# Moving weight preparation on GpSimd: into the f and v loop, and behind the first image's value sums

## The chip, the cores and the metric

The kernel runs on one core of a Trainium2 chip. The metric is the device time of one execution in microseconds (us). The engines are named as in the profile: PE is TensorE's matrix products, PEld its weight loads, DVE is VectorE, ACT is ScalarE, POOL is GpSimd and SP is SyncE, whose queue issues most of the DMAs. Each engine works through its own queue of instructions in the order in which the program issued them.

## What is computed

The input is four images of 256 channels and 64 x 64 points, in float32. Two layers follow each other. The reference, cut to what matters here:

```python
# layer 0: attention over the 4096 points of an image
attn = softmax(einsum('bnd,bdm->bnm', q, k), axis=-1)
x = gamma[0] * einsum('bcn,bmn->bcm', v, attn) + x

# layer 1, cluster: f and v are 1x1 convolutions of the normed image to 96 channels,
# folded into 2 x 2 quarters of 4 heads, 4 centres in each
cn = cen * rsqrt((cen * cen).sum(-1) + 1e-12)
pn = pts * rsqrt((pts * pts).sum(-1) + 1e-12)      # pts are the points of f
sim = sigmoid(beta + alpha * einsum('bmc,bnc->bmn', cn, pn))
mask = one_hot(argmax(sim, axis=1))                # one centre for each point
sim = sim * mask
agg = (einsum('bmn,bnc->bmc', sim, v2) + v_cen) / (mask.sum(-1) + 1.0)
y = x + ls1 * conv1x1(einsum('bmn,bmc->bnc', sim, agg), proj_w)

# layer 1, the multilayer part
hdn = conv1x1(gelu(conv1x1(group_norm(y), mlp_w1)), mlp_w2)   # 256 -> 1024 -> 256
y = y + ls2 * hdn
z = relu(batch_norm(y * dw_w))
z = relu(batch_norm(conv1x1(z, pw_w)))
```

## The kernel before

The order of the work is written out by hand: the whole body stands under `tc.manual_schedule()` (line 2052), so each engine receives its instructions in the order in which the Python code issues them. Waits between engines are placed by what reads and writes which tile.

Several matrix products are done with fewer multiplications, by seven products of quarters in place of eight. This needs sums and differences of the quarters of both factors. Those of the weights are made by POOL, in place where the room allows it:

- `turn_mlp` (line 248) does two instructions on the first weights of the multilayer part, tile `w1`: it adds the quarter D to C (line 251) and multiplies D by -1 (line 252).
- `turn_w2` (line 1622) does three on the second weights, tile `w2`: lines 1627, 1629 and 1631. The results w7 and s2 go to buffers of the tags `rden` and `q`; s1 overwrites a quarter of `w2` in the first three images and has a buffer of its own in the last.
- The last step of `load_rest` (line 176) does two on `wpw_s`, the weights of the closing convolution (lines 188 and 189).

For an image the work runs in this order:

1. `alone` (line 865), for the first image only: projections, the scores of the first block of points, and the values v in pairs (`v_pair`). `added(g)` issues four POOL sums over v each, through the helper at line 664. The generator `load_rest` is stepped from u = 3 on: its first four steps issue the DMAs of the remaining weights on SP's queue, the fifth is the subtraction in `wpw_s`. Behind the loop follow `added(5)`, `added(6)`, `exps(0)`, `factors(0)`, `added(7)`. `exps(u)` subtracts the maximum on DVE and takes the exponential on ACT; `factors(u)` makes sums of quarters of the exponentials, one on DVE (line 678, tile t) and the others on POOL (line 664, tiles s, t and acc).
2. `weighting`: 64 units of scores times values. POOL and DVE make the sums of quarters, TensorE multiplies (line 734). Near its end `load_mlp` issues the DMAs of w1 and w2 on SP's queue. In the last image `turn_mlp` is called right at its end.
3. `cluster` (line 1140). After the group norm comes the f and v loop (line 1319) over eight blocks of 512 points. For each, TensorE makes f and v (line 1331) in one of two PSUM buffers, DVE moves them to SBUF with their bias (line 1341) and the similarities too (line 1350). `heads(nb - 1)` squares f of the block before on POOL (line 1310; for the last block line 1308) and sums the squares on DVE (line 1312). In the loop's block 6 the first half of the similarities is finished (`similar(0)`).
4. Behind the loop DVE works through the two halves of the masks: `affine` (line 1268), `largest` (lines 1273 to 1281), `weights` (line 1286), with `similar(1)` in between (line 1261). `fill(n)` hands TensorE pieces of other work meanwhile, the value projections of the next image (line 443) or, in the last image, the last block of the image before. Then TensorE sums the values by masks (`summed`, line 1366), the counts follow, and `turn()` is called at line 1398, which is five POOL instructions, or three in the last image. Behind it in the code stand the transposes (line 1412), two small POOL memsets (1423, 1424) and the product named gp (line 1434).
5. `mlp`: the multilayer part, which reads what `turn()` made.

The call that the change moves, and the one that steps `load_rest`:

```python
        summed(lambda j, q: sim[:, j, q, :], False)
        count(0)
        count(1)
        turn()
...
                if u > 2:
                    next(rest, None)
```

Of the kernel before, what the change touches and what calls it, by code (L numbers as in the profile page):

```python
# [11 lines left out]
ALU = mybir.AluOpType  # L12
# [48 lines left out]
def attention_then_cluster_block(  # L61
# [17 lines left out]
    nc = tc.nc  # L79
# [168 lines left out]
    def turn_mlp():  # L248

        _, w_cd, _, w_d = own_w["q"]  # L250
        nc.gpsimd.tensor_tensor(w_cd, w_cd, w_d, ALU.add)
        nc.gpsimd.tensor_scalar(w_d, w_d, -1.0, None, ALU.mult)

    def roots():
        for s, v in ((dw_d, "dw_v"), (pw_s, "pw_v")):
            rsqrt(s, par(v), BN_EPS)
        table(AF.Exp)
# [80 lines left out]
    def attention(b, xs, ys):  # L338
# [54 lines left out]
        def staged():  # L393

            st = spool.tile([P, 4, NB], F32R, tag="s", name=f"st_{b}")
            ps = ps_s.tile([P, 2, NB], F32, tag="s", name=f"pr_{b}")
            k0, q0 = (st[:, 0], st[:, 1]), (st[:, 2], st[:, 3])
            for j, w in enumerate("kq"):  # L400
                projected(w, 0, ps[:, j])
            halves_of("k", *k0, ps[:, 0])
            k_straight(0, k0)
            qs[0] = work.tile([P, NB], F32R, tag="q", name=f"q_{b}_0")
            halves_of("q", *q0, ps[:, 1])
            straight("q", 0, qs[0], *q0, nc.scalar)
            for u in range(1, 4):
                k_straight(u, k0)
            return k0, q0
# [43 lines left out]
        def v_pair(i):  # L453
            for j in range(2 * i, 2 * i + 2):
                for k in range(KC):
                    v_step(j, k)
# [408 lines left out]
        def alone():  # L865

            roots()
            for i in range(2):
                v_pair(i)
            k0, q0 = staged()  # L870
            for i in range(2, 5):
                v_pair(i)

            def added(*gs):
                for g in gs:
                    for f in sums(g):
                        f()

            added(0, 1)
            rest = load_rest()  # L880
            for u in range(GRP):
                half(u, 0)()
                if u < GRP - 1:
                    half(u, 1)()
                else:

                    sc = products(u, 1)
                    highest_of(0, tiles(sc))
                    kept(u, 1, sc)
                if u == 0:  # L890
                    k1 = halved("k", 1, False)
                    for i in range(4, GRP):
                        k_straight(i, k1)
                elif u == 1:
                    q1 = halved("q", 1, False)
                else:
                    v_pair(u + 3)
                    if u % 2 == 0:
                        added(u // 2 + 1)
                if 1 < u < 6:  # L900
                    written("kqkq"[u - 2], (u - 2) // 2, *(k0, q0, k1, q1)[u - 2], nc.gpsimd)
                if u == 3:
                    q_block(1)
                    k_unit(GRP)
                if u > 2:
                    next(rest, None)
            fold(0)
            v_pair(11)
            added(5)
            tp = turned_over(0, ps_m.tile([P, 4, P], F32, tag="m", name=f"tt_{b}_0"))  # L910
            half(GRP, 0)
            v_pair(12)
            dgs["dg"] = across(0, "w2", tp)
            v_pair(13)
            added(6)
            spread(0, dgs["dg"])
            v_pair(14)
            wf()
            exps(0)
            factors(0)  # L920
            v_pair(15)
            half(GRP, 1, True)
            added(7)
            for _ in rest:
                pass
# [32 lines left out]
        def weighting(next_x, fill, early, begin):  # L958
# [125 lines left out]
            for _ in range(4):  # L1084
                next(quarters)
            if b == B - 1:
                turn_mlp()
            table(AF.Sqrt)
            ends = b == B - 1
            fill(1 if ends else 2)  # L1090
# [49 lines left out]
    def cluster(b, ys, stats, cells, rest, fill, gelu, nxt, maxima, turn):  # L1140
# [161 lines left out]
        def heads(nb, between=lambda: None):  # L1302

            fh, o = nb // 4, nb % 4
            f = vf[nb // 2][:, nb % 2, :, :ED]
            for g in range(2) if nb == NBLK - 1 else ():
                h = f[:, 2 * g : 2 * g + 2]
                nc.gpsimd.tensor_tensor(h, h, h, ALU.mult)
            if nb < NBLK - 1:
                nc.gpsimd.tensor_tensor(f, f, f, ALU.mult)  # L1310
            between()
            nc.vector.tensor_reduce(
                prns[fh].rearrange("p (q j h) -> p q j h", q=2, j=8)[:, :, 2 * o : 2 * o + 2],
                f.rearrange("p (g j) (h e) -> p g j h e", g=2, h=HEADS),
                AX.X,
                ALU.add,
            )

        for nb in range(NBLK):
            fh, o = nb // 4, nb % 4  # L1320
            if 1 < nb + 1 < NBLK:
                norm(nb + 1)
            if nb in later:
                later[nb]()
            xn = xns.pop(nb)

            ps = ps_s.tile([P, 2, 2, C], F32, tag="s", name=f"fv_{b}_{nb}")
            for j in range(4):
                g = j // 2
                for k in range(KC):  # L1330
                    nc.tensor.matmul(  # L1331
                        ps[:, g, j % 2, : 2 * ED + 16],
                        xn[:, k, j * P : (j + 1) * P],
                        mix[:, k, fh, 16 * g : 16 * g + 2 * ED + 16],
                        start=(k == 0),
                        stop=(k == KC - 1),
                    )
            if nb == NBLK - 1:
                heads(nb - 1)
            for g in range(2):  # L1340
                nc.vector.tensor_tensor(
                    vf[nb // 2][:, nb % 2, 2 * g : 2 * g + 2, :],
                    ps[:, g, :, 16 - 16 * g : 16 - 16 * g + 2 * ED],
                    fvb.unsqueeze(1).to_broadcast([P, 2, 2 * ED]),
                    ALU.add,
                )
            for g in range(2):
                q = 2 * fh + g
                d0 = 2 * ED * g
                nc.vector.tensor_tensor(  # L1350
                    folded(sgs[fh])[:, g, 2 * o : 2 * o + 2],
                    ps[:, g, :, d0 : d0 + 16],
                    dot_b[:, q * 16 : (q + 1) * 16].unsqueeze(1).to_broadcast([P, 2, 16]),
                    ALU.add,
                )
            if 0 < nb < NBLK - 1:
                heads(nb - 1)
            if nxt and nb == 2:
                nxt.queries()

        agg_p = ps_a.tile([P, NB], F32, tag="a0", name=f"agg_{b}")

        def summed(w, first):
# [31 lines left out]
        summed(lambda j, q: sim[:, j, q, :], False)  # L1395
        count(0)
        count(1)
        turn()

        cnt_p = ps_a.tile([P, NB], F32, tag="a1", name=f"cnt_{b}")  # L1400
        nc.tensor.matmul(cnt_p[:ED, :64], ones[:, :ED], bests[0], start=True, stop=True)
# [217 lines left out]
        t = own_w["w2"]  # L1619
        return t[:, :h_n, :P], t[:, h_n:, :P], t[:, :h_n, P:], t[:, h_n:, P:]  # L1620

    def turn_w2(b, kept):


        a11, _, a21, a22 = quarters_w2()
        w7 = work.tile([P, h_n, P], F32, tag="rden", bufs=1, name=f"w2_7_{b}")
        nc.gpsimd.tensor_tensor(w7, a21, a11, ALU.subtract)
        s1 = work.tile([P, h_n, P], F32, tag="q", name=f"w2_1_{b}") if kept else a21
        nc.gpsimd.tensor_tensor(s1, a21, a22, ALU.subtract)
        s2 = work.tile([P, h_n, P], F32, tag="q", name=f"w2_2_{b}")  # L1630
        nc.gpsimd.tensor_tensor(s2, s1, a11, ALU.subtract)
        return s1, s2, w7

    def mlp(b, ys, stats2, fill, nxt, blocks, turned, maxima):

# [416 lines left out]
    with tc.manual_schedule():  # L2052
        here = attention(0, xs0, [])
        here.alone()
        late = None
        for b in range(B):
            xs1 = []
            nxt = attention(b + 1, xs1, []) if b + 1 < B else None

            def next_x():  # L2060
                if nxt:
                    xs1.append(load_x(b + 1, len(xs1)))

            begin, todo, gelu = late or (
                lambda: None,
                list(nxt.projections) if nxt else [],
                lambda i: None,
            )
            fill = filler(todo)
            stats, cells, rest = here.weighting(  # L2070
                next_x, fill, [] if b else derived(), begin
            )
            turned = []

            def turn():
                if nxt:
                    turn_mlp()
                turned.extend(turn_w2(b, not nxt))

            maxima = []  # L2080
            stats2 = cluster(b, here.ys, stats, cells, rest, fill, gelu, nxt, maxima, turn)

            late = mlp(b, here.ys, stats2, fill, nxt, NBLK - (b == B - 2), turned, maxima)
            here = nxt
# [76 lines left out]
```

## Time and profile before

| | |
|---|---|
| median of three runs | 3128.08 us (3124.45 to 3131.26) |
| profiled execution, its own time | 3132.96 us |
| its span in the profile | 3131.2 us |
| mean granted clock of TensorE | 0.994 |
| PE busy | 3052.7 us (97%) |
| DVE busy | 2513.3 us (80%) |
| POOL busy | 2330.7 us (74%) |
| ACT busy | 1780.1 us (57%) |
| `turn()`, five POOL instructions, image 0 | 565.93 to 572.96 us, 1.26 to 1.54 us each |
| the subtraction in `wpw_s`, two POOL instructions | 58.62 to 59.72 us |

A row of a timeline gives the start in us, the duration in us, the engine, the line of the kernel, the operation, what it writes and reads, the shapes, and how many instructions are merged in it; a bracket at the end gives the idle time of the engine just before it and who ended it. A row of the waits gives who waited for whom, the total in us, how often, and the longest. A row of the chain of waits gives start, duration, engine, tile and line of one piece of the chain that ended last. Rows of stages give the stage, its length, and the busy time and number of instructions of PE, PEld, DVE, ACT and POOL, then the granted clock of TensorE as a share of full speed, the DMA share and GB/s.

### The profile page before, as it was taken

What the parts mean: (1) busy time and instruction counts of PE and PEld (TensorE: products, weight loads), DVE (VectorE), ACT (ScalarE), POOL (GpSimd) and SP (SyncE); (2) the same over time, 40 slices, a digit from 0 to 9 for tenths busy, and PEclk for the clock granted to TensorE, in tenths of its full rate; (3) what the DMA queues carried; (4) which work ended last, traced back from release to release, by engine and by line L of the source; (5) the groups of instructions that cost most, each with busy time, mean ns of one, the idle gap of its engine ahead of it and who ended that gap; (6) DMA issues with size and microseconds to landing.
All of it is one profiled execution on the core that took longest, in us unless ns stands there. A gap on an engine that the chain in (4) does not pass through costs nothing.

```text
span 3131.2 us, 41360 instructions
## 1 busy us (share of the span) xinstructions
PE 3052.7 (97%) x14210; PEld 2498.0 (80%) x14210; DVE 2513.3 (80%) x3548; ACT 1780.1 (57%) x2817; POOL 2330.7 (74%) x2243
## 2 busy tenths in 40 slices
PE   8999999999999999999999999999999999999999
PEld 5788887788688888878868888886877888875886
DVE  4999888777798888877779888877768988887675
ACT  5666664544566666454556666645446666655444
POOL 5888886477588888657758888955766988893563
PEclk9999999999999999999999999999999999999999
DMA  5112226100112113510011212440011112150000
GB/s 174 47 56 64 61 90 168 58 18 28 48 47 68 55 61 111 157 44 26 19 58 44 68 61 64 117 144 34 28 41 44 59 57 67 55 153 1 14 21 28
DMA packets 105570, 200.40 MB, mean 64 GB/s; under 512 B 14880, under 2 KB 30864, under 8 KB 103824
## 3 DMA queue, kind: packets, MB, share of 16 engines
q1 hardware_dynamic: 100464, 178.66, 17.9%
q0 software_dynamic: 4256, 18.90, 2.9%
q8 instruction: 113, 1.85, 0.2%
q14 instruction: 97, 0.79, 0.1%
q10 hardware_dynamic: 640, 0.20, 0.0%
HBM read 147.01 MB, written 48.34 MB: 62 GB/s over the span
## 4 chain that ended last, share of the span: by engine, by line
PE 73%; DVE 9%; POOL 9%; issue 3%; ACT 3%; DMA 2%; SPq 1%; POOLq 0%; ACTq 0%; DVEq 0%
PE av L734 34%; PE mo L1771 10%; PE sc L489 7%; PE hq L1854 5%; PE hp L1854 3%; PE hr L1854 3%; PE fv L1331 3%; POOL acc L664 3%; POOL t L664 2%; DVE top L513 2%; DVE s L655 2%; PE vp L443 2%; POOL s L664 1%; PE mo L1755 1%; PE hq_pw L1854 1%
## 5 line engine op out<-in xcount | busy, mean ns | idle before, releaser
L502 ACT COPY s<-sc 128x1024 f32<-128x1024 f32 x512 | 515.2, 1012 | 426.3 <-PE sc L489 418.2
L655 DVE TENSOR_TENSOR s<-s,hold 128x1024 f32<-128x1024 f32 x512 | 598.5, 1209 | 9.9 <-ACT hold L638 6.0
L664 POOL TENSOR_TENSOR acc<-acc,t 128x512 f32<-128x512 f32 x408 | 541.9, 1348 | 0.0
L734 PE MATMUL av<-s,sum 128*128 128x256 f32 x2048 | 527.1, 380 | 5.5 <-POOL s L664 5.3
L734 PE MATMUL av<-t,v 128*128 128x256 f32 x2048 | 527.2, 380 | 2.5 <-POOL t L664 2.4
L734 PE MATMUL av<-s,v 128*128 128x256 f32 x2048 | 525.7, 379 | 2.5 <-ACT t L764 1.3
L664 POOL TENSOR_TENSOR s<-t,s 128x512 f32<-128x512 f32 x256 | 341.9, 1336 | 221.9 <-DVE t L678 154.9
L678 DVE TENSOR_TENSOR t<-s,hold 128x1024 f32<-128x1024 f32 x256 | 311.7, 1217 | 189.4 <-POOL acc L664 98.1
L513 DVE TENSOR_TENSOR top<-sc,top 128x1024 f32<-128x1024 f32 x350 | 426.6, 1219 | 21.4 <-ACT s L502 17.6
L734 PEld LDWEIGHTS av<-s,v 128*128 128x128 f32 x2048 | 387.3, 189 | 65.0 <-ACT xn L1722 2.3
L734 PEld LDWEIGHTS av<-s,sum 128*128 128x128 f32 x2048 | 387.7, 190 | 63.7 <-POOL s L664 11.4
L734 PEld LDWEIGHTS av<-t,v 128*128 128x128 f32 x2048 | 387.4, 190 | 63.4 <-POOL t L664 8.9
L1809 ACT ACTIVATE hs<-hs,pv_s 128x256 f32<-128x256 f32 x496 | 232.6, 503 | 353.2 <-DVE hs L1845 353.2
L489 PE MATMUL sc<-q,k 128*128 128x512 f32 x1024 | 392.8, 468 | 20.0 <-ACT s L502 9.6
L1771 PE MATMUL mo<-hs,w 128*128 128x256 f32 x1512 | 385.0, 381 | 0.0
L664 POOL TENSOR_TENSOR t<-s 128x512 f32<-128x512 f32 x256 | 330.3, 1290 | 45.4 <-PE av L734 31.8
L1771 PEld LDWEIGHTS mo<-hs,w 128*128 128x128 f32 x1512 | 283.7, 190 | 47.3 <-ACT hs L1809 6.2
L659 ACT ACTIVATE hold<-s 128x512 f32<-128x512 f32 x256 | 154.2, 602 | 214.9 <-DVE s L655 214.7
L1845 DVE TENSOR_TENSOR hs<-hq,hs 128x256 f32<-128x256 f32 x496 | 198.5, 421 | 86.6 <-PE hq L1854 76.2
L661 ACT ACTIVATE s<-s 128x1024 f32<-128x1024 f32 x256 | 266.9, 1043 | 0.0
L734 PE MATMUL av<-t,sum 128*128 128x256 f32 x1024 | 262.4, 378 | 0.0
L489 PEld LDWEIGHTS sc<-q,k 128*128 128x128 f32 x1024 | 174.2, 189 | 108.2 <-DVE top L513 59.1
(292 smaller groups left out, 4878.5 us busy)
## 6 DMA issues: line engine op xcount, KB each, us to landing
k<-k SPq DMA_DIRECT2D x248, 256.0 KB, 2.7
x<-in_x SPq DMA_DIRECT2D x62, 512.0 KB, 6.9
out<-xn SPq DMA_DIRECT2D x62, 256.0 KB, 2.1
att<-t SPq DMA_DIRECT2D x56, 256.0 KB, 4.0
x<-att POOLq DMA_DIRECT2D x12, 1024.0 KB, 9.9
w<-in_w SPq DMA_DIRECT2D x8, 1024.0 KB, 11.8
q<-q SPq DMA_DIRECT2D x31, 256.0 KB, 4.1
rden<-row_rd SPq DMA_DIRECT2D x28, 256.0 KB, 3.7
```

The lines of the kernel that those rows point to most:

```text
L489: nc.tensor.matmul(sc[:, r, :], k_s[:, (2 * h + r) * P : (2 * h + r + 1) * P], qs[u // GRP], start=True, stop=True,)
L502: nc.scalar.copy(slots[u][:, PAIR[h]].rearrange("p h r n -> p r h n"), tiles(sc))
L513: nc.vector.tensor_tensor(top, src, top if saved[nb] is None else saved[nb], ALU.max)
L655: nc.vector.tensor_tensor(sh, sh, mb.to_broadcast([P, 2, 2, QW]), ALU.subtract)
L661: nc.scalar.activation(s[:, PAIR[1]], s[:, PAIR[1]], AF.Exp)
L664: nc.gpsimd.tensor_tensor(out, x, y, op)
L678: nc.vector.tensor_tensor(t31[u], s[:, B11 : B22 + 1 : 2], b12.to_broadcast([P, 2, 2, QW]), ALU.add)
L734: nc.tensor.matmul(av[bank][:, half_ * QW : (half_ + 1) * QW], a[:, r], t[:, r], start=(g == 0 and r == 0 and i in (1, 7, 2, 4)), stop=(g ...
L1771: return nc.tensor.matmul(bank[:, half * HB : (half + 1) * HB], a[:, j], t, start=start, stop=stop)
L1809: nc.scalar.activation(src, src, AF.Gelu_apprx_tanh, bias=pvc("b1", P, j + 4 * (i > 1)))
L1845: nc.vector.tensor_tensor(dst, ps, term, ALU.add)
L1854: nc.tensor.matmul(out, w, x, start=True, stop=True)
```

## The change

`turn_mlp` and `turn_w2` become generators that yield after each POOL instruction. `cluster` makes one generator of both ahead of the f and v loop and takes one step of it behind `heads(nb - 1)` in the blocks 1 to 6; what is left is run out behind the loop, and the call behind the counts is gone. The last image's call of `turn_mlp` at the end of `weighting` stays where it was. In `alone`, `load_rest` is stepped four times in place of five, so that the subtraction in `wpw_s` is issued by the loop at the end of `alone`, behind `added(7)`. No instruction is added or taken away.

```diff
--- before.py
+++ after.py
@@ -248,8 +248,8 @@
     def turn_mlp():
 
         _, w_cd, _, w_d = own_w["q"]
-        nc.gpsimd.tensor_tensor(w_cd, w_cd, w_d, ALU.add)
-        nc.gpsimd.tensor_scalar(w_d, w_d, -1.0, None, ALU.mult)
+        yield nc.gpsimd.tensor_tensor(w_cd, w_cd, w_d, ALU.add)
+        yield nc.gpsimd.tensor_scalar(w_d, w_d, -1.0, None, ALU.mult)
 
     def roots():
         for s, v in ((dw_d, "dw_v"), (pw_s, "pw_v")):
@@ -902,8 +902,8 @@
                 if u == 3:
                     q_block(1)
                     k_unit(GRP)
-                if u > 2:
-                    next(rest, None)
+                if 2 < u < 7:
+                    next(rest)
             fold(0)
             v_pair(11)
             added(5)
@@ -1084,7 +1084,8 @@
             for _ in range(4):
                 next(quarters)
             if b == B - 1:
-                turn_mlp()
+                for _ in turn_mlp():
+                    pass
             table(AF.Sqrt)
             ends = b == B - 1
             fill(1 if ends else 2)
@@ -1316,6 +1317,8 @@
                 ALU.add,
             )
 
+
+        turning = turn()
         for nb in range(NBLK):
             fh, o = nb // 4, nb % 4
             if 1 < nb + 1 < NBLK:
@@ -1355,9 +1358,12 @@
                 )
             if 0 < nb < NBLK - 1:
                 heads(nb - 1)
+                next(turning, None)
             if nxt and nb == 2:
                 nxt.queries()
 
+        for _ in turning:
+            pass
         agg_p = ps_a.tile([P, NB], F32, tag="a0", name=f"agg_{b}")
 
         def summed(w, first):
@@ -1395,7 +1401,6 @@
         summed(lambda j, q: sim[:, j, q, :], False)
         count(0)
         count(1)
-        turn()
 
         cnt_p = ps_a.tile([P, NB], F32, tag="a1", name=f"cnt_{b}")
         nc.tensor.matmul(cnt_p[:ED, :64], ones[:, :ED], bests[0], start=True, stop=True)
@@ -1619,17 +1624,17 @@
         t = own_w["w2"]
         return t[:, :h_n, :P], t[:, h_n:, :P], t[:, :h_n, P:], t[:, h_n:, P:]
 
-    def turn_w2(b, kept):
+    def turn_w2(b, kept, turned):
 
 
         a11, _, a21, a22 = quarters_w2()
         w7 = work.tile([P, h_n, P], F32, tag="rden", bufs=1, name=f"w2_7_{b}")
-        nc.gpsimd.tensor_tensor(w7, a21, a11, ALU.subtract)
+        yield nc.gpsimd.tensor_tensor(w7, a21, a11, ALU.subtract)
         s1 = work.tile([P, h_n, P], F32, tag="q", name=f"w2_1_{b}") if kept else a21
-        nc.gpsimd.tensor_tensor(s1, a21, a22, ALU.subtract)
+        yield nc.gpsimd.tensor_tensor(s1, a21, a22, ALU.subtract)
         s2 = work.tile([P, h_n, P], F32, tag="q", name=f"w2_2_{b}")
-        nc.gpsimd.tensor_tensor(s2, s1, a11, ALU.subtract)
-        return s1, s2, w7
+        yield nc.gpsimd.tensor_tensor(s2, s1, a11, ALU.subtract)
+        turned.extend((s1, s2, w7))
 
     def mlp(b, ys, stats2, fill, nxt, blocks, turned, maxima):
 
@@ -2074,8 +2079,8 @@
 
             def turn():
                 if nxt:
-                    turn_mlp()
-                turned.extend(turn_w2(b, not nxt))
+                    yield from turn_mlp()
+                yield from turn_w2(b, not nxt, turned)
 
             maxima = []
             stats2 = cluster(b, here.ys, stats, cells, rest, fill, gelu, nxt, maxima, turn)
```

## Prediction

> **What bounds the kernel now.** I read the page first, then the chain of waits, then the timelines of the stretches that the change touches.
>
> ```profile
> PE 3052.7 (97%) x14210; PEld 2498.0 (80%) x14210; DVE 2513.3 (80%) x3548; ACT 1780.1 (57%) x2817; POOL 2330.7 (74%) x2243
> PEclk9999999999999999999999999999999999999999
> ```
>
> TensorE is busy for 97% of the span, so only two things can shorten the run: less idle time on TensorE, or no time at a lower clock. The change touches POOL alone; it is worth something only where POOL makes TensorE wait. The waits of the stretch behind f and v in the first image (564 to 577 us), and the stages of it, show such a place:
>
> ```profile
> PE agg L1366 <- DVE sim L1286: 3.7, 1, 3.7
> ...
> 565.90:572.90 7.00, 6.45 (x89) 5.20 (x88) 6.83 (x11) 5.19 (x8) 6.75 (x6) 1.00 0.00 0
> 572.90:576.10 3.20, 0.05 (x4) 0.05 (x8) 2.99 (x8) 0.39 (x2) 0.34 (x3) 0.76 0.02 5
> 574.60:581.20 6.60, 5.15 (x72) 4.86 (x73) 3.49 (x10) 0.82 (x2) 0.00 (x0) 0.50 0.00 0
> ```
>
> The columns are the stage, its length, busy time of PE, PEld, DVE, ACT, POOL, then the granted clock. TensorE has 0.05 us of work in 3.2 us while DVE is full: DVE's chain over the masks sets the time. And the clock is 0.50 from 574.6 to 581.2, long after the work is back. That chain, with POOL beside it:
>
> ```profile
> 568.83 0.42 DVE L1280 TENSOR_REDUCE scr<-scr 128x64 f32<-128x256 f32 x1
> 569.29 1.14 DVE L1281 TENSOR_TENSOR scr<-scr 128x256 f32<-128x256 f32 x1
> 570.46 1.38 DVE L1286 TENSOR_TENSOR sim<-sg,scr 128x256 f32<-128x256 f32 x1
> 571.76 1.49 DVE L1268 TENSOR_SCALAR sg<-sg 128x256 f32<-128x256 f32 x1
> ...
> 575.11 0.42 DVE L1281 TENSOR_TENSOR scr<-scr 128x256 f32<-128x256 f32 x1
> 575.57 0.43 DVE L1286 TENSOR_TENSOR sim<-sg,scr 128x256 f32<-128x256 f32 x1
> ...
> 568.88 1.26 POOL L1627 TENSOR_TENSOR w<-w 128x512 f32<-128x512 f32 x1
> 570.22 1.34 POOL L1629 TENSOR_TENSOR w<-w 128x512 f32<-128x512 f32 x1
> 571.64 1.32 POOL L1631 TENSOR_TENSOR w<-w 128x512 f32<-128x512 f32 x1
> ```
>
> The same DVE instructions take 0.42 and 0.43 us six us later, when POOL is done. Each long one ends just after a POOL instruction of turn() ends. In the last image turn() has three steps, which end at 2863.64; there the long ones are L1261 (0.91) and L1277 (1.49), and L1281, L1286 and L1268 behind them take 0.43, 0.42 and 0.28. So the excess follows turn(), not the line.
>
> Where the steps would go, POOL looks like this in the f and v loop (the bracket is its idle time before):
>
> ```profile
> 546.53 0.83 POOL L1310 TENSOR_TENSOR vf<-vf 128x384 f32<-128x384 f32 x1 [1.92 <-DVE vf L1341]
> 549.41 0.83 POOL L1310 TENSOR_TENSOR vf<-vf 128x384 f32<-128x384 f32 x1 [2.05 <-DVE vf L1341]
> ```
>
> At the start of the run POOL stands for 8 us in front of work that could run:
>
> ```profile
> 58.62 0.46 POOL L188 TENSOR_TENSOR wpw_s<-wpw_s 128x128 f32<-128x128 f32 x1 [8.05 <-DMA wpw_s<-in_wpw]
> 59.18 0.54 POOL L189 TENSOR_SCALAR wpw_s<-wpw_s 128x128 f32<-128x128 f32 x1
> ...
> 65.94 2.25 POOL s L664
> ```
>
> The last line is from the chain of waits: it runs over POOL from 58.62 to 79.59.
>
> **Part 1: turn() into the f and v loop.** Nothing is added or removed: five POOL instructions (three in the last image), no DMA. They move on POOL's queue ahead of the squares heads(1) to heads(7); the two memsets L1423 and L1424 move up with the gap. SP's queue is untouched.
>
> *Gain at the old place.* Images 0 to 2: L1281 1.14 - 0.42, L1286 1.38 - 0.42, L1268 1.49 - 0.28, so 0.72 + 0.96 + 1.21 = 2.89 us each. L1275 (0.59 for 0.42) I leave out: L226 behind it waits for ACT's root, which ends at 567.42. The tanh that L1268 needs ends at 569.43, before DVE would come there (570.2), so it does not take over. What is late next is TensorE's own filler: it ends at 572.0 and the first four agg matmuls at 572.35; the masks then come at 576.00 - 2.89 = 573.1. A gap of 0.8 us stays and the whole 2.89 counts: 3 x 2.89 = 8.7. Last image: 0.49 + 1.07 = 1.56 on DVE, but TensorE's gap there is only 1.41, so 1.4. Sum 10.1.
>
> *Clock.* In the last image, with a gap of 1.41 us, the clock stays 1.00. From the first agg matmul after the gap to the gp matmul takes 3.42 us there; images 0 to 2 have one small filler piece in that way (0.43 us warm): TensorE's work is 1.51 + 0.31 + 0.44 + 0.25 + 0.45 + 0.43 = 3.39, and I take 3.45. By the chain it now takes 5.78 (576.05 to 581.83), 6.04 (1350.34 to 1356.38) and 4.86 (2123.18 to 2128.04). With a gap of 0.8, less than the 1.41 that left the clock alone, that returns 2.33 + 2.59 + 1.41 = 6.3 us. [...]
>
> *Cost at the new place.* Each step must fit between two squares. The gaps are 1.92, 2.05, 3.97, 2.05, 1.92; the steps 1.33, 1.54, 1.26, 1.34, 1.32. The tightest is the second, 2.05 - 1.54 = 0.5 to spare. Cover beyond that: heads(0) ends at 544.61 and its reduce L1312 on DVE starts at 546.57, 1.96 later, and DVE then idles 1.14 per block. So cost nothing; if that cover were gone, a late square would hold DVE, the eviction behind it, and TensorE for want of a PSUM buffer. Does POOL now hold DVE there? [...] In the loop DVE runs L1341 and L1350 (one input from PSUM) and reduces. L1341 takes 0.55 us in all 64 cases, those beside the POOL square L1308 included; the reduces L1273 and L1312 kept 0.42 and 0.54 under L251. [...] Bounds for the new place: 0, and 0.2 us for each of 18 steps if L1341 were held 1.3 (it has 1.14 to spare): 3.6. I take 0.
>
> *Added wait.* POOL now needs w1 and w2 at 544.6 instead of 565.9. They are issued at 508.5 and 509.8 and land within 15.6 us, by 525.4: 19 us early. Buffers rden and q have no reader after 528.2.
>
> **Part 2: the first image's subtraction.** The two instructions (0.46 + 0.54, 1.1 with gaps) move behind twelve sums and factors(0)'s three. The DMA of wpw is still issued where it was, so SP is unchanged. POOL is then free from 50.57; the sums can run as v arrives (copies end at 52.4, 57.2, 62.6), and the first factor s waits for DVE t, which ends at 63.40: 65.94 becomes 63.45, 2.5 us earlier. The 1.1 us comes back before the next s (75.71), so 1.4 is left there and at 79.51, where DVE t waited 5.24 us for POOL. TensorE's gaps there for POOL's s are 1.19 and 0.59, so it can use it. Ends: nothing, if DVE's blocked turns fall worse; 4, if POOL's stretched rows (2.25, 2.27, 1.59) go as well. I take 1.4.
>
> **Sum.** 10.1 + 6.3 + 1.4 = 17.8 us. The profiled execution took 3132.96 (span 3131.2, so 1.8 around it): 3115.2. It lies 4.9 above the median of the three runs shown, so on that footing 3128.08 - 17.8 = 3110.3.
>
> **Rivals.** [...] (b) DVE's long rows are not POOL's doing, or return elsewhere, so only part 2 is left: 3126.7. Against: the last image, where they moved with turn(). (c) Slower: POOL's step holds the square behind it, the reduce, the eviction and TensorE. It decides when a step exceeds its gap by the 0.5 + 1.96 + 1.14 = 3.6 above, that is at 5.1 us; to end 0.2% slower it must cost (17.8 + 6.3) / 18 = 1.3 us per step beyond: steps of 6.5 us, and 3134.4. Nothing in the trace stretches a POOL instruction of that size past 2.32.
>
> **How the numbers follow.** Forecast 0.72, (a) 0.15, (b) 0.08, (c) 0.05. About 0.2% (6.3 us) is what a measurement of this kernel can tell from no change. Forecast and (a) are faster: 0.87; (b) the same: 0.08; (c) slower: 0.05. The forecast's ends are a gain of 8.7 + 4.2 - 1 = 12 and 10.1 + 7.8 + 4 = 22, that is 3106 to 3116; with (a) and a run's scatter of 3 us: 3103 to 3120.
>
> **What would show it.** Right: L1281, L1286 and the second L1268 at 0.42, 0.42 and 0.28 in all images; PE's wait for L1286 at about 0.8 us, 60 agg matmuls in 1.5 us, no 0.5 clock behind them; POOL's idle before L1310 at 0.5 to 0.7; L188 without a wait, the first s at 63.5. Wrong: DVE waiting for L1310 in the loop, L1341 over 0.6, or the 0.5 clock still there.

## The result, and the profile after

| | before | after |
|---|---|---|
| median of five runs each | 3128.49 us (3124.45 to 3133.66) | 3112.69 us (3112.12 to 3117.37) |
| span of the profiled execution | 3131.2 us | 3110.9 us |
| mean granted clock of TensorE | 0.994 | 0.998 |

The changed kernel takes 0.995 of the time before, with an interval of 0.9937 to 0.9964: 15.8 us less by the medians. The predicted saving was 17.8 us. The two profiled executions differ by 20.3 us, because that of before lay 4.5 us above its median; so the sizes below are taken from anchors inside the traces. In the trace of before the clock was at 0.50 for 20.5 us outside the three gaps (from 598.48, 2827.38, 2888.82 and 2899.06 us on), in that of after for 10.2 us ahead of the last 1.5 us of its span, in which TensorE does nothing. What those 10.2 us of difference cost is, as an estimate, at most half of them, 5.1: at 0.50 the 60 products shown below take 2.78 us for 1.51.

The line numbers have moved by one to six: L1281 of before is L1282 now, L1286 is L1287, L1268 is L1269, L1310 is L1311, L1341 is L1344, L1366 is L1372, L1434 is L1439.

From the page, and from the waits of the stretch behind f and v in the first image (535 to 580 us), and a stage of it:

```profile
PE 3042.2 (98%) x14210; PEld 2488.0 (80%) x14210; DVE 2501.5 (80%) x3548; ACT 1779.4 (57%) x2817; POOL 2327.7 (75%) x2243
```

```profile
PE agg L1372 <- DVE sim L1287: 1.0, 1, 1.0
```

```profile
572.00:582.00 10.00, 9.50 (x107) 6.18 (x109) 6.42 (x13) 4.64 (x11) 2.17 (x2) 1.00 0.00 0
```

DVE's busy time is 11.8 us less with the same number of instructions; its count is the same 3548. TensorE waits 1.0 us for the masks where it waited 3.7, and the granted clock is 1.00 throughout: in the whole trace of after it falls for the first time at 2870.47 us, behind the last image's masks. DVE's timeline of that stretch shows the chain over the masks:

```profile
568.10 0.42 DVE L1281 TENSOR_REDUCE scr<-scr 128x64 f32<-128x256 f32 x1
568.55 0.42 DVE L1282 TENSOR_TENSOR scr<-scr 128x256 f32<-128x256 f32 x1
569.01 0.43 DVE L1287 TENSOR_TENSOR sim<-sg,scr 128x256 f32<-128x256 f32 x1
569.35 0.29 DVE L1269 TENSOR_SCALAR sg<-sg 128x256 f32<-128x256 f32 x1
...
571.50 0.42 DVE L1282 TENSOR_TENSOR scr<-scr 128x256 f32<-128x256 f32 x1
571.96 0.42 DVE L1287 TENSOR_TENSOR sim<-sg,scr 128x256 f32<-128x256 f32 x1
```

The rows that took 1.14, 1.38 and 1.49 us are at 0.42, 0.43 and 0.29. POOL's timeline shows where the steps are now, each behind one square, with POOL's idle time before the square in the bracket:

```profile
542.91 0.82 POOL L1311 TENSOR_TENSOR vf<-vf 128x384 f32<-128x384 f32 x1 [20.51 <-DVE vf L1344]
543.70 1.27 POOL L251 TENSOR_TENSOR w<-w 128x512 f32<-128x512 f32 x1
545.66 0.83 POOL L1311 TENSOR_TENSOR vf<-vf 128x384 f32<-128x384 f32 x1 [0.70 <-DVE vf L1344]
546.46 1.49 POOL L252 TENSOR_SCALAR w<-w 128x512 f32<-128x512 f32 x1
548.54 0.83 POOL L1311 TENSOR_TENSOR vf<-vf 128x384 f32<-128x384 f32 x1 [0.59 <-DVE vf L1344]
```

The squares still wait for DVE, not for POOL: 0.70 and 0.59 us of slack are left. TensorE's timelines of the same image, before and after, give two anchors of the sums below, the first products with the masks behind the gap and gp:

```profile
576.05 2.78 PE L1366 MATMUL agg<-vf,sim 128*32 128x96 f32 x60 [3.71 <-DVE sim L1286]
...
581.67 0.60 PE L1434 MATMUL gp<-wproj_s,scr 97*128 97x256 f32 x2
```

```profile
572.44 1.51 PE L1372 MATMUL agg<-vf,sim 128*32 128x96 f32 x60 [1.00 <-DVE sim L1287]
...
575.86 0.67 PE L1439 MATMUL gp<-wproj_s,scr 97*128 97x256 f32 x2
```

Last, POOL's timeline at the start of the run:

```profile
64.38 1.29 POOL L664 TENSOR_TENSOR s<-t,s 128x512 f32<-128x512 f32 x1 [3.84 <-DVE t L678]
...
66.98 2.26 POOL L664 TENSOR_TENSOR acc<-s 128x512 f32<-128x512 f32 x1
...
70.00 1.72 POOL L664 TENSOR_TENSOR v<-v 128x256 f32<-128x256 f32 x1
...
73.31 0.45 POOL L188 TENSOR_TENSOR wpw_s<-wpw_s 128x128 f32<-128x128 f32 x1
73.85 1.39 POOL L189 TENSOR_SCALAR wpw_s<-wpw_s 128x128 f32<-128x128 f32 x1
75.22 1.26 POOL L664 TENSOR_TENSOR s<-t,s 128x512 f32<-128x512 f32 x1
```

The subtraction (L188, L189) no longer waits for its DMA, and the first factor s starts 1.56 us earlier than before (65.94). But the second s starts only 0.49 us earlier (75.71): L189 takes 1.39 in place of 0.54.

### The profile page after: what moved, and what is told of

It is laid out like the page before. It is cut to its first block, busy times and chain, and to the rows that moved or that the text cites. A ratio compares the mean times of both kernels' runs of the same rounds, so it can differ in the third digit from the quotient of the medians.

```text
span 3110.9 us, 41355 instructions
## 1 busy us (share of the span) xinstructions
PE 3042.2 (98%) x14210; PEld 2488.0 (80%) x14210; DVE 2501.5 (80%) x3548; ACT 1779.4 (57%) x2817; POOL 2327.7 (75%) x2243
## 4 chain that ended last, share of the span: by engine, by line
PE 74%; DVE 9%; POOL 8%; issue 3%; ACT 3%; DMA 2%; SPq 1%; POOLq 0%; ACTq 0%; DVEq 0%
PE av L734 34%; PE mo L1776 10%; PE sc L489 7%; PE hq L1859 5%; PE hp L1859 3%; PE hr L1859 3%; PE fv L1334 3%; POOL acc L664 3%; DVE s L655 2%; POOL t L664 2%; DVE top L513 2%; PE vp L443 1%; POOL s L664 1%; PE mo L1760 1%; DMA w<-in_w 1%
## 5 line engine op out<-in xcount | busy, mean ns | idle before, releaser
L513 DVE TENSOR_TENSOR top<-sc,top 128x1024 f32<-128x1024 f32 x350 | 426.6, 1219 | 21.6 <-ACT s L502 18.0
```

The source lines that it names most:

```text
L513: nc.vector.tensor_tensor(top, src, top if saved[nb] is None else saved[nb], ALU.max)
```

## The experiments

### Each part alone

One kernel has part 1 only, that is, the old stepping of `load_rest` is restored in the changed kernel:

```diff
-                if 2 < u < 7:
-                    next(rest)
+                if u > 2:
+                    next(rest, None)
```

> Part 1 alone: turn() in the f and v loop, the subtraction in wpw_s where it was. My theory (POOL's lock on DVE and the halved clock behind the gap) puts nearly all of the gain here: 15 to 16.5 us less than before (15.5 by the anchors of the two traces: 4.9, 5.2, 4.0 and 1.4 us in the four images), and no 0.5 clock behind the masks. If the gain came from the start of the run, it is near 0.

The other has part 2 only: the same edit the other way round, in the kernel before.

> Part 2 alone: the subtraction in wpw_s behind the value sums, turn() where it was. My theory: 0.5 to 1.5 us less than before, within what can be told from no change; POOL no longer waits for the DMA of wpw_s, the first s near 63.5 us, L1281, L1286 and L1268 still at 1.14, 1.38 and 1.49. A rival in which POOL's earlier start is carried through to the end gives 2.5 to 4 us.

Measured side by side: part 1 alone 3114.26 us, 0.9951 of before (0.9939 to 0.9964); part 2 alone 3130.01 us, 1.0003 (0.9995 to 1.0011), with before at 3129.71. So the loop accounts for the gain, 15.4 us, and part 2 gives nothing that can be measured: the bound of its interval leaves at most 1.6 us. POOL's timeline of part 2 alone:

```profile
64.53 1.28 POOL L664 TENSOR_TENSOR s<-t,s 128x512 f32<-128x512 f32 x1 [3.84 <-DVE t L678]
...
70.15 1.73 POOL L664 TENSOR_TENSOR v<-v 128x256 f32<-128x256 f32 x1
...
73.47 1.54 POOL L188 TENSOR_TENSOR wpw_s<-wpw_s 128x128 f32<-128x128 f32 x1
75.11 0.54 POOL L189 TENSOR_SCALAR wpw_s<-wpw_s 128x128 f32<-128x128 f32 x1
75.63 1.26 POOL L664 TENSOR_TENSOR s<-t,s 128x512 f32<-128x512 f32 x1
```

The second s starts at 75.63, which is 0.08 us before the 75.71 of the kernel before. The first s starts 1.41 us earlier than before (65.94), not 2.5, since DVE's t ends at 64.45 in this run and not at 63.40. From the first s to the second it is 11.10 us where it was 9.77: s itself is no longer stretched (1.28 for 2.25), but the subtraction takes 2.16 with its gaps where it took 1.1, because L188 is stretched now (1.54 for 0.46). The stretch has moved, not gone.

### The gap filled, POOL left as it was

If part of the gain is the clock's, then it must be possible to have that part without touching POOL. Into the kernel before come three products of 128x512 on TensorE, which nothing reads, behind `fill`, in the place of the idle gap. DVE and POOL stay as they are.

```diff
         fill(5 if nxt else 4)
+        if nxt:
+            warm = ps_a.tile([P, NB], F32, tag="a1", name=f"warm_{b}")
+            for _ in range(3):
+                nc.tensor.matmul(
+                    warm, ones, wv_s.rearrange("p k m -> p (k m)"), start=True, stop=True
+                )
```

> The kernel before with three added products in images 0 to 2 whose result nobody reads (2.8 us of TensorE's time), put ahead of the agg products that wait for the masks. DVE stays held by POOL, the gap on TensorE falls from 3.7 to about 1 us. If the clock follows TensorE's gap, the 0.5 clock goes away and the run is 6.3 us shorter (4.2 to 7.8) though TensorE has more to do and L1281, L1286 and L1268 are as long as before. If the clock has another cause, or the gain is DVE's alone, no change (or slower by what the products take).

Measured: 3123.91 us, 0.9984 (0.9977 to 0.999) of before, which is 5.8 us less, by work that is added. TensorE's timeline, and a stage behind it (each of the three products is two instructions in the row):

```profile
569.79 2.74 PE L1390 MATMUL warm<-wv_s,ones 128*128 128x512 f32 x6
572.46 0.36 PE L1366 MATMUL agg<-vf,sim 128*32 128x96 f32 x4
573.98 1.51 PE L1366 MATMUL agg<-vf,sim 128*32 128x96 f32 x60 [1.16 <-DVE sim L1286]
```

```profile
573.00:582.00 9.00, 7.96 (x96) 5.44 (x97) 5.34 (x13) 3.63 (x7) 0.63 (x1) 1.00 0.00 0
```

The masks come as late as before relative to the work ahead of them, but the gap is 1.16 us and the 60 products take 1.51, not 2.78. So this part is the clock's, and what is left of part 1's 15.4 us, 9.6, is that of DVE's shorter chain. The anchors of the two traces of before and after divide the gain in the same way: from the 60 products to gp the three images took 5.62, 5.85 and 4.70 us and take 3.42 now, 5.9 less in all; the rest is 2.74, 2.73, 2.74 and, in the last image, 1.42, which is 9.6.

### The gap reopened without POOL

The reverse: in the changed kernel, where no POOL work lies beside the masks, DVE gets six unread reduces in the first three images.

```diff
         weights(0)
         affine(1)
+        for _ in range(6 if nxt else 0):
+            nc.vector.tensor_reduce(rc, quad(sgs[1]), AX.X, ALU.max)
```

> The changed kernel with six added reduces on DVE in images 0 to 2 whose result nobody reads (0.46 us each, 2.75 us in all) between the two halves of the masks. POOL holds nobody; the gap on TensorE is 3.75 us again. If the gap alone makes the clock fall, the 0.5 clock is back and the run is 8.2 us of DVE plus about 6 us of clock = 14 us longer than the changed kernel. If the clock's fall came from the blocking between POOL and DVE, 8 us.

Measured: 3126.69 us, 0.9992 (0.9983 to 1.0) of before; against 3112.69 for the changed kernel that is 14.0 us more, and 12.4 more than part 1 alone, which ran beside it. TensorE's timeline and a stage:

```profile
576.22 2.77 PE L1372 MATMUL agg<-vf,sim 128*32 128x96 f32 x60 [3.59 <-DVE sim L1287]
```

```profile
576.00:580.00 4.00, 3.78 (x66) 3.51 (x67) 1.56 (x5) 0.24 (x1) 0.00 (x0) 0.50 0.00 0
```

A wait of 3.59 us with POOL at 0.00 in the stage brings the 0.50 back. Three gaps that are 2.59 us longer are 7.8 us. From the 60 products to gp it is 5.79, 4.69 and 4.89 us in the three images, where 3.42 is the time at full clock: 5.1 more, and 12.9 with the gaps. So the clock's part is 4.6 to 6.2 by the medians and 5.1 by the trace, about what the prediction put on it. The whole is well above the 8 us expected if the gap alone did not lower the clock.

### How long a gap is too long

The same reduces, two in the first image, three in the second, four in the third. This kernel ran once.

```diff
-        for _ in range(6 if nxt else 0):
+        for _ in range((2, 3, 4, 0)[b]):
```

> The changed kernel with two, three and four added unread DVE reduces in images 0, 1 and 2, so gaps on TensorE of 1.9, 2.4 and 2.8 us in place of 1.0. Gaps of 1.0 and 1.4 left the clock at 1.00, gaps of 3.6 and 3.7 halved it in every image. [...] The total is about 4 us above the changed kernel by DVE's work, and up to 6 more by the clock.

Measured: 3121.55 us. TensorE's timelines of the three images, and two stages behind the second and the third gap:

```profile
574.26 1.51 PE L1372 MATMUL agg<-vf,sim 128*32 128x96 f32 x60 [1.77 <-DVE sim L1287]
...
1343.09 2.77 PE L1372 MATMUL agg<-vf,sim 128*32 128x96 f32 x60 [2.23 <-DVE sim L1287]
...
2113.89 2.50 PE L1372 MATMUL agg<-vf,sim 128*32 128x96 f32 x60 [2.69 <-DVE sim L1287]
```

```profile
1344.00:1346.00 2.00, 2.00 (x45) 1.72 (x38) 0.02 (x1) 0.09 (x1) 0.00 (x0) 0.50 0.00 0
...
2114.00:2116.00 2.00, 2.00 (x58) 2.00 (x59) 0.83 (x2) 0.00 (x0) 0.00 (x0) 0.56 0.04 8
```

A wait of 1.77 us left the clock alone, waits of 2.23 and 2.69 halved it. By the profile's record of the granted clock it stayed low for 3.41 us behind both (from 1342.82 and 2114.23 us on). Behind the wait of 3.59 us in the reopened gap it stayed low for 6.83 us in the first image and for 3.41 in the next two.

The same record shows where it falls. In the kernel before, the three falls behind the gaps come at 574.58, 1349.41 and 2124.24, for 6.83, 6.83 and 3.41 us; the first two are 774.83 us apart, 227 times 3.4133, and the other falls of that trace, those of after and those of the graded gaps also lie whole multiples of 3.413 us apart within their trace. What sets this grid was not shown. Counted from the falls of the graded gaps, the windows of 3.41 us, from one point of the grid to the next, in which most of each wait lies are these (the third column is PE's busy time):

```profile
571.41:574.82 3.41, 1.64 (x36) 1.07 (x38) 3.24 (x9) 2.04 (x3) 0.00 (x0) 1.00 0.02 5
1339.41:1342.82 3.41, 1.45 (x10) 0.82 (x8) 3.17 (x9) 2.07 (x3) 0.00 (x0) 1.00 0.00 0
2110.82:2114.23 3.41, 0.72 (x21) 0.48 (x24) 3.24 (x8) 1.36 (x2) 0.00 (x0) 1.00 0.00 0
```

With 1.64 us of TensorE's work in the window the clock stayed, with 1.45 and 0.72 it fell at the window's end. Around the masks the windows of the other traces read here divide in the same way: it fell behind those with 1.18, 0.65 and 1.05 us of work in the kernel before, and not behind the 2.42 in each of the first three images of after. Elsewhere the division is not so sharp: in the trace of before the clock fell behind a window with 1.98 us of work (595.06 to 598.47) and stayed at 1.00 behind windows with 1.57 (226.42 to 229.83), with 1.39 and, at the very start, with 0.00 (4.55 to 7.97 and 1.14 to 4.55). So the author's reading is that a gap counts by what it takes from one window, not by its length alone.

### More work in the loop

Behind each step of the loop POOL gets one more unread addition (128x512, 1.03 us), and in a second kernel two. This asks how much room the loop really had.

```diff
-                next(turning, None)
+                if next(turning, None) is not None:
+                    if nb == 1:
+                        own_w["extra"] = work.tile([P, NB], F32, tag="w2", ...)
+                    v2 = wv_s.rearrange("p k m -> p (k m)")
+                    for _ in range(1):        # the second kernel: range(2)
+                        nc.gpsimd.tensor_tensor(own_w["extra"], v2, v2, ALU.add)
```

> The changed kernel with one added POOL instruction (128x512, two reads, 1.27 us, result unread) behind each step in the f and v loop. A block of POOL is then 0.83 + 1.3 + 1.3 = 3.4 us against the loop's 2.81 per block, so POOL falls behind by 0.6 us a block, and catches up 2 us in the block with the query projection. By the 1.96 us of lead that a square has on its reduce, plus DVE's 1.14 of idle time, nothing is lost: the changed kernel's time within 2 us, L1313 waiting for POOL at most a little. If POOL's instructions slow DVE's evictions in the loop, some microseconds are lost and L1344 is longer than 0.56.

> The same with two added POOL instructions behind each step: 4.7 us per block of POOL against 2.81. Priced per step, as the prediction's slower rival was (a step of 3.9 us, harmful only from 5.1 on), nothing is lost. Priced as a backlog that runs up over the blocks, POOL is 1.9 us later with each, past the 3.1 of cover by the second block: 4 us later at the last square in images 0 to 2, and 12 to 20 us above the changed kernel in all.

Measured: with one 3113.1 us, 0.9945 (0.9931 to 0.9958), nothing lost; with two 3124.35 us, 0.998 (0.9971 to 0.9989), 11.7 us over the changed kernel and 11.3 over the one with one addition; that is just under the 12 to 20 us that a backlog was priced at, and far from the nothing of the price per step. L1344, the eviction on DVE, has a median of 552 ns with one and 548 ns with two, against 554 ns in the changed kernel: POOL's work in the loop doesn't hold this instruction. POOL's timeline with two, the waits of that stretch, and TensorE's timeline in the second and the third image:

```profile
548.48 0.83 POOL L1311 TENSOR_TENSOR vf<-vf 128x384 f32<-128x384 f32 x1
549.28 1.50 POOL L252 TENSOR_SCALAR w<-w 128x512 f32<-128x512 f32 x1
550.76 2.15 POOL L1366 TENSOR_TENSOR xt<-wv_s 128x512 f32<-128x512 f32 x2
552.87 0.83 POOL L1311 TENSOR_TENSOR vf<-vf 128x384 f32<-128x384 f32 x1
```

```profile
DVE prn L1313 <- POOL vf L1311: 3.6, 4, 1.7
```

```profile
1347.16 2.78 PE L1377 MATMUL agg<-vf,sim 128*32 128x96 f32 x60 [1.81 <-DVE sim L1287]
...
2120.29 1.51 PE L1377 MATMUL agg<-vf,sim 128*32 128x96 f32 x60 [1.81 <-DVE sim L1287]
```

The squares have no bracket any more: POOL runs without a pause. One square and one tripled step are 4.1 to 4.4 us, while the squares of before follow each other every 3.22 us in the mean (546.53 to 562.65, five periods). So POOL falls about one us further behind in each block, and the reduce L1313 waits 3.6 us in four places in the first image. With one addition the period's work is 3.0 to 3.3 us, just what the period holds. The price follows from the anchors: against the changed kernel the first agg products with `pool_w` come 1.44 us later in the first image (the start of the run), then 4.09, 9.76 and 12.37 us later in the next three. That is 2.65, 5.67 and 2.61 us an image; the middle one holds 3.4 us at half clock (the 2.78 above for 1.51, and the small products behind: 4.89 us from the 60 products to gp for 3.42), which is 1.5; another 1.6 of it was not traced to its place. The same wait, 1.81 us, left the clock alone in the first and the third image and halved it in the second. The windows of 3.41 us, on the grid of the one fall at 1347.02, show a difference:

```profile
572.19:575.61 3.42, 2.02 (x11) 1.01 (x9) 3.18 (x9) 3.00 (x6) 0.00 (x0) 1.00 0.02 5
1343.60:1347.02 3.42, 1.42 (x8) 0.82 (x8) 3.18 (x9) 2.26 (x4) 0.00 (x0) 1.00 0.00 0
2118.43:2121.85 3.42, 1.61 (x63) 1.42 (x62) 2.68 (x6) 0.57 (x3) 0.00 (x0) 1.00 0.02 5
```

In the first image a point of the grid, at 575.61, divides the wait (574.69 to 576.50), 2.02 us of work are left in the window ahead of it, and the clock stayed. In the third the whole wait lies in one window with nothing else idle, 1.61 us of work are left, and it stayed. In the second most of it falls together with a third of a us of other idle time, 1.42 are left, and it fell.

### The subtraction somewhere else

Part 2 put the subtraction behind the sums; this puts it into the f and v loop of the first image, behind the five steps.

```diff
                 yield from turn_w2(b, not nxt, turned)
+                if b == 0:
+                    nc.gpsimd.tensor_tensor(pw_q[1], pw_q[1], pw_q[3], ALU.add)
+                    nc.gpsimd.tensor_scalar(pw_q[3], pw_q[3], -1.0, None, ALU.mult)
```

(and the same two lines leave `load_rest`)

> The changed kernel with the subtraction in wpw_s taken out of the start and put into the sixth block of the first image's f and v loop (POOL idle for 1.5 us there, the two take 1.1; first read in the multilayer part). At the start two POOL instructions that take 1.9 to 2.2 us with DVE's blocking are gone ahead of the second s, on which DVE and TensorE wait: 1 to 2 us less than the changed kernel. If the start is set by the landing of k and not by POOL, no change.

Measured: 3112.56 us, 0.9945 (0.9932 to 0.9959): not to be told from the changed kernel. From the end of the first t to the start of the first `acc<-t,t` it is 12.47 us in place of 13.48, 1.0 less, as expected there; but two traces with one and the same start differ by 0.9 in this stretch (see the start, below), so the microsecond is not shown, and it can't be seen at the end.

### The gap that is left

A gap of 1.00 us is left in images 0 to 2. One more piece of filler, four products that take 0.87 us, fits into it:

```diff
-        fill(5 if nxt else 4)
+        fill(6 if nxt else 4)
```

> The changed kernel with one more piece of filler (0.92 us of TensorE's work) ahead of the products that wait for the masks, in images 0 to 2, taken from what is flushed later. The gap of 1.0 us that the change leaves falls to 0.1: up to 3 x 0.9 = 2.7 us less than the changed kernel if the later places can spare the piece; no change or slower if a later wait (the group norms' one) is then uncovered.

A second kernel has this and the subtraction in the loop, and the changed kernel ran again beside both.

> The longer filler together with the subtraction of wpw_s in the f and v loop. Alone the latter gave nothing that can be told; so the same as with the longer filler alone, 0 to 3 us less than the changed kernel.

> The changed kernel again, on the same chip as the two with longer filler, so that these can be compared: within 3 us of 3112.7.

Measured: the changed kernel 3115.71 us, 3.0 above its first median, 0.9956 (0.9942 to 0.9969); with the longer filler 3126.33, 0.9987 (0.9979 to 0.9996); with both 3125.85, 0.9984 (0.9975 to 0.9993). The filler costs 10.6 us, where a gain of up to 2.7 was hoped for and a loss named as possible; with both, a gain was expected and the same loss came. From the trace of the longer filler, TensorE's timeline and a stage further on, and DVE's timeline there:

```profile
600.79 0.80 PE L1859 MATMUL hp<-xn,w 128*128 128x256 f32 x2 [2.62 <-issue]
```

```profile
600.00:610.00 10.00, 8.58 (x32) 4.95 (x33) 5.50 (x14) 2.46 (x6) 0.00 (x0) 0.66 0.27 97
```

```profile
595.68 0.16 DVE L226 RECIPROCAL rstd_gn<-rstd_gn 128x1 f32<-128x1 f32 x1 [0.91 <-ACT rstd_gn L224]
598.97 0.75 DVE L369 SCALAR_TENSOR_TENSOR hl_k<-kp,bqk_s,hl_k 128x512 fp32r<-128x512 f32 x1 [3.12 <-ACT hl_k L368]
599.63 0.22 DVE L326 TENSOR_SCALAR ga_gn<-pc_s,rstd_gn 128x2 f32<-128x2 f32 x1
```

The pieces come from one supply. Taken early, one is missing under the second group norm, and the next thing in line, the projection of k, moves up into that place. Its move out of PSUM (L369) now stands on DVE's queue between L226 and L326 of the group norm and waits 3.12 us for ACT. TensorE starts the multilayer part with 2.62 us of nothing, and the clock drops to 0.66 in the mean of the next 10 us, which is again 6.8 us at 0.50. The same 2.62 stands in the second image, with 6.8 us at 0.50 behind it (a clock of 0.66 in the mean of 1370 to 1380 us).

So the last kernel takes the piece from another cover, the `fill(3)` behind the next image's q and k:

```diff
-        fill(5 if nxt else 4)
+        fill(6 if nxt else 4)
...
         nxt.q_block(0)
         nxt.k_unit(0)
-        fill(3)
+        fill(2)
```

> The longer filler ahead of the masks' products, with the piece taken from the filler that stands behind the cluster's last products (three pieces become two), so that the group norm behind it keeps all of its own. If the loss of the longer filler came only from the uncovered group norm, its 2.6 us of waiting and the halved clock are gone. Gain over the changed kernel: by TensorE alone up to 2.7 us; but in the changed kernel DVE's statistics run without a break to 593.05 and the group norm's first product starts at 593.70, so DVE takes over and I expect 0 to 1 us.

Measured: 3112.43 us, 0.9949 (0.9935 to 0.9962), the same as the changed kernel. TensorE's timeline:

```profile
571.76 2.01 PE L1372 MATMUL agg<-vf,sim 128*32 128x96 f32 x64
...
597.46 0.67 PE L1859 MATMUL hp<-xn,w 128*128 128x256 f32 x2 [0.43 <-ACT probe L299]
```

The gap is gone (all 64 products run in one piece), but hp starts at 597.46 where it starts at 597.67 in the changed kernel: 0.2 us earlier, with DVE's chain of statistics ahead of it in both. The last products with the masks end 0.2 us earlier too (573.77 for 573.95), so the masks still set that end; where the 0.87 us of work that is saved later turns into waiting again was not followed. No version that ran is faster than the changed kernel by more than their scatter.

## Why the prediction was right, point by point

**The stretched rows (10.1 us).** Right, and all three images show it: each of the three rows fell to the predicted value, and POOL's idle before the squares behind a step fell to 0.59 to 0.76 (2.74 in the block with the query projection), where 0.5 to 0.7 was expected. The gap is 1.00 us, not 0.8. The share of the stretched rows alone, part 1 less the filled gap, is 15.4 - 5.8 = 9.6 us, and 9.6 by the anchors. That the stretch is POOL's doing is shown by the undoing: the same DVE instructions stand in the same order, and only POOL's place changed. Not every DVE row beside POOL was long: in the trace of before L1261 took 0.42 us from 568.04 on, beside the tensor_scalar L252 (567.36 to 568.90).

**The clock (6.3 us).** Right. The filled gap gave 5.8 us (3.1 to 7.2 by its interval) with DVE and POOL as they were, and the reopened gap took 4.6 to 6.2 without POOL. The half clock comes with TensorE's idle gap, and a gap of 2.23 us sufficed. The prediction gave 0.15 to a clock that falls all the same, with 11.5 us of gain; at a gap of 1.0 us it did not fall. The windows that hold this gap whole have 2.42 us of work in each of the three images, and the fullest window ahead of a fall in the trace of before held 1.98. At 1.81 us one gap of three did harm. The 6.3 itself was read from one execution, and another differs: in the trace of part 2 alone, with the same three gaps, the clock stayed low for 6.83, 3.41 and 3.41 us, and the three stretches are 4.8 longer than at full clock in place of 5.9. That the value came out so near is in part luck. The prediction's ends, 4.2 and 7.8, were an estimate, three times the smallest and three times the largest of its three terms, 1.41 and 2.59; no run shows either of them, and what the runs showed, 5.8, 4.6 to 6.2 and 5.9 by the anchors, lies between.

**Both together, by image.** From the first products with `pool_w` to gp the changed kernel is shorter by 4.94, 5.16, 4.02 and 1.42 us (images 0 to 3), 15.5 in all. The prediction's terms by image, 2.89 + 2.33, 2.89 + 2.59, 2.89 + 1.41 and 1.4, are 5.22, 5.48, 4.30 and 1.4, 16.4 in all. The 0.3 that each of the first three lacks has two halves. Up to the 60 products they gain 2.74, not 2.89: in the first image DVE's first L1269, which stands beside the last square on POOL in both kernels, takes 0.76 for 0.62. And the stretch from there to gp is 3.42 us as predicted (3.45), but its old length was read in the chain at 581.83, 0.16 behind gp's start in the timeline (581.67), and 0.19 and 0.16 behind it in the next two images.

**The start (1.4 us).** Not shown, and probably too large: "The 1.1 us comes back before the next s (75.71), so 1.4 is left there". Part 2 alone gives nothing that can be measured (1.0003, 0.9995 to 1.0011), though up to 1.6 us lie within that interval, so the 1.4 is not excluded. The sum took 1.1 us for the subtraction at its new place; there it meets DVE's L513 (73.32 to 74.84 in the changed kernel) and takes 1.9 to 2.2. And it took the end of DVE's t as fixed at 63.40; in the changed kernel t ends at 64.30, and in part 1 alone, whose start is that of before, at 65.44. The lower end of the prediction's own bounds, "nothing, if DVE's blocked turns fall worse", fits best. The two profiled executions of before and after by themselves would have confirmed the 1.4: from the end of the first t to the first `acc<-t,t` it is 14.88 us in one and 13.48 in the other. But part 1 alone, with the old start, has 13.94, and part 2 alone 13.75: two runs with the same start differ by 0.9, so one pair of traces can't tell.

**The cost in the loop (0).** Right as a value: L1344 stays at 0.55 us, and even a second addition per step is free. Wrong as a threshold. Rival (c) said that a step does harm from 5.1 us on, from the covers of a single step (0.5 + 1.96 + 1.14). With two additions the step is 3.4 to 3.65 us, still below 5.1, and the run is 11.7 us longer. What the sum left out is that the covers are used once while the delay adds up from block to block: the right comparison is POOL's work per block (square and step) against the block's period, 3.22 us.

**The sum.** 17.8 predicted, 15.8 measured by the medians and 15.4 in later runs of the same kernel. The difference is of the size of the start's 1.4 and the 0.9 between the 16.4 and the 15.5, and also of the scatter: the interval of the measured gain is 11.3 to 19.7 us.

## What to carry to other kernels

When an instruction has two durations in one trace (here 0.42 and 1.14 us for L1281), look at what the other engines do during the long one; here work that nothing waited for until much later stretched a chain that everything waited for. In these runs a gap on TensorE had two prices, its length (2.74 us of it in each of three images) and the clock behind it (5.9 us in all three), and cut to 1.00 us, behind which the clock did not fall, it paid the second price back whole. Before work is put into a loop, compare the queue's whole work per period with the period, and before a filler is lengthened, find out whose cover it is taken from.

## What the hardware showed that was not expected

- The clock halved behind waits of 2.23 and 2.69 us (graded gaps) and 3.59 (gap reopened), behind one of three of 1.81 (two additions per step), and not behind 1.77 (graded gaps), 1.41 (last image of before), 1.16 (gap filled) and 1.00 (after).
- Behind a wait it stayed low for 3.41 us or for 6.83: 3.41 behind 1.81, 2.23 and 2.69, 6.83 behind the 2.62 in front of the multilayer part, and either of the two behind 3.59 and 3.7. The falls of the traces of before, of after and of the graded gaps lie, each trace for itself, on one grid of 3.413 us. Around the masks the clock fell where a window of that grid held 0.65 to 1.45 us of TensorE's work, and not at 1.61 or more; a window with 1.98 elsewhere in the trace of before had a fall behind it too.
- Both engines' rows were stretched. Where a DVE instruction had started first, POOL's additions took 2.25 to 2.27 us for 1.28 (before: 65.94 and 69.50; after: 66.98), and its small ones 1.73 for 0.73 (part 2 alone: 70.15) and 1.39 for 0.54 (after: 73.85). In part 2 alone, where the two start within 0.01 us of each other (73.47 and 73.48), POOL's took 1.54 for 0.46.
- Adding 2.74 us of useless products on TensorE in each of three images made the run 5.8 us shorter.
